# A graph-attention layer: adjacency pieces placed between the loads of x tiles, and the first table's rows stored from GpSimd's queue

## The chip, the cores and the metric

The kernel runs on one core of a Trainium2 chip. The metric is the device time of one execution in microseconds (us). A core has five engines with instruction queues of their own: TensorE (PE in the profile, its weight loads PEld), VectorE (DVE), ScalarE (ACT), GpSimd (POOL) and SyncE (SP). Each works through its queue in order. In this program SP, ACT and POOL also issue DMAs, which 16 shared DMA engines carry out. In the profile SPq and ACTq are the moments in which those queues issue a DMA.

## What is computed

The reference is one layer of graph attention with a residual and a layer norm, on x of 8 batches x 2048 nodes x 64 channels and one adjacency matrix of 2048 x 2048 for all batches, cut here to what matters:

```python
def _gat_layer(h, mask, b):
    scores = jnp.einsum('...nd,...md->...nm', h, h)
    scores = jnp.where(mask, scores, NEG)
    attn = jax.nn.softmax(scores, axis=-1)
    return jnp.einsum('...nm,...md->...nd', attn, h) + b
mask = graph + jnp.eye(N, dtype=graph.dtype) > 0
h = jnp.einsum('bnc,hdc->bhnd', x, Wh)                  # 4 heads of 64
out_h = _gat_layer(h, mask[None, None], bh[None, :, None, :])
z = leaky_relu(concat of the heads)
h2 = jnp.einsum('bnk,dk->bnd', z, Wo)
out2 = _gat_layer(h2, mask[None], bo)
x = layernorm(x + layernorm(leaky_relu(out2)) * gamma + beta)
```

The adjacency matrix is sparse. Only the first 32 nodes ("hubs") have many neighbours.

## The kernel before

`fast_kernel` works on the sparse matrix. (`general_kernel`, a dense version, runs only when a flag at the end says that a list of neighbours did not fit. It does not run here.) The nodes behind the 32 hubs are put into 168 sets of 12. For each set the kernel finds, on the chip, the nodes that any of the 12 is linked to, at most 128. It gathers their rows from a table in DRAM by an indirect DMA and does the attention of the set on them alone. The first attention layer gathers from `table1`, the second from `table2`, which the first one writes.

The work stands in three parts. The opening is from the start to about 142 us. The first layer runs over pairs of sets from there to about 640 us, and the second layer to the end. The change touches the opening, which does the following.

- **x tiles.** x is read in 16 tiles of 128 nodes with all 8 batches. `load_x(i)` (lines 462 to 467) sets two columns of ones on DVE and issues two DMAs of 128 KB from ACT's queue. `save_x(i)` (lines 469 and 470) stores the tile as 128 rows of 520 floats (260 KB) into `table1`, from ACT's queue too. Ten tile buffers go round.
- **Adjacency pieces.** `load_adj(r, t, m)` (lines 674 to 699) reads one piece: 120 rows (ten sets) by 1024 columns, by two or three DMAs from SP's queue, one of 440 KB and small ones (lines 681 and 682). POOL then turns the integers into a bf16 mask (line 687, about 1.1 us). After the second half m = 1 it sets the diagonal by small selects (lines 695 and 698). The raw integers use three buffers, the masks five. There are 34 pieces, in three rounds r of up to 60 sets. A piece is named below as round, ten and half. Where the round is 0 it is left out, so 5_1 is the second half of the sixth ten of round 0. `more(n)` issues the next n of them.
- **Hubs.** `hub_mask`, `hub_mask_sets`, `weights` and `hub_columns` prepare the hubs' masks and weights. In the x loop, `hub_scores(i)` computes the hubs' scores against tile i: matmuls (line 602), a subtraction of the mask on DVE (605) and an exponential on ACT (607). `turn_x(i + 1)` transposes the next tile on PE (525), and ACT copies it out (595). `hub_values(i - 1)` sums on PE (618). In step 3 POOL also sets a number of small tiles (lines 972 to 980) and builds the powers for a last short ten (`make_powers6`, line 713).
- **Picking neighbours.** `make_keys(r, t3, ...)` multiplies the masks of three tens by powers of two on PE (729), and DVE makes keys of them (718). Step 2 of the loop needs pieces 0_0 to 2_1 for it, step 6 pieces 3_0 to 5_1. From step 6 on, `pick(0)` hands out jobs to DVE, four in each step: MAX8 and match-replace (745, 747) pick the largest keys. `pick(0)` also issues, on POOL, a memset of the buffer `cand` (741), which the first MAX8 needs.
- **End of the opening.** After the loop come the keys of round 1 and the first six gathers on POOL (804), which need the whole of `table1`. Then `own_rows` runs on POOL, and the first matmul of the first layer (819, tile `cat`) at 142.05 us.

The order is written out by hand: under `manual_schedule` each engine gets its instructions in program order. Every DMA of SP and ACT carries one of eight completion semaphores, given out in rotation in program order. Before a DMA is issued its queue waits for the earlier user of that semaphore. DMAs of POOL have eight of their own. So a load of x waits for adjacency DMAs that stand some eight DMAs ahead of it in the program. While it waits, nothing behind it on ACT's queue runs.

The loop of the opening, before the change (lines 949 to 970):

```python
    more(6)
    hub_mask()
...
    turn_x(0)
    hub_columns()
    more(4)
...
    for i in range(NB):
        if i + 4 < NB:
            load_x(i + 4)
        more(1 if i >= 6 else 0)
        save_x(i)
```

Of the kernel before, what the change touches and what calls it, by code (L numbers as in the profile page):

```python
# [359 lines left out]
def fast_kernel(ctx: ExitStack, tc: tile.TileContext, x, adj, Wh, bh, Wo, bo, gamma, beta, out, flag):  # L360


    nc = tc.nc
    B, N, C = x.shape
    H, D, _ = Wh.shape
    P = 128
# [61 lines left out]
    table1 = dram.tile([N, ROW], F32, name="table1")  # L428
# [22 lines left out]
    xrow = {}  # L451
# [10 lines left out]
    def load_x(i):  # L462
        t = xrow[i] = rows_tile(f"x{i}")
        nc.vector.memset(t[:, :, 0:PW:PW - 1], 1.0)
        for p in range(2):
            nc.scalar.dma_start(out=t[:, :, 1 + p * D:1 + (p + 1) * D],
                                in_=x[p::2, i * P:(i + 1) * P, :].rearrange("q n c -> n q c"))

    def save_x(i):
        nc.scalar.dma_start(out=table1[i * P:(i + 1) * P, :], in_=xrow[i].rearrange("n q c -> n (q c)"))  # L470

    NCH = HALFN
    in_round = [min(FIRST, NS - FIRST * r) for r in range(NR)]
# [77 lines left out]
    def hub_mask():  # L551
        for k in range(2):
            nc.vector.tensor_scalar(hubm[:, k * NCH:(k + 1) * NCH], hubraw[k], 1.0, 0.0, OP.min, OP.max)
        nc.vector.tensor_tensor(hubm[:, :HUB], hubm[:, :HUB], identb[:HUB, :HUB], OP.max)
        pm = two("pm")
        for m in range(NB):
            nc.tensor.matmul(pm[:, m // 8, (m % 8) * HUB:(m % 8 + 1) * HUB], hubm[:, m * P:(m + 1) * P],
                             identb[:HUB, :HUB], start=True, stop=True)
        for k in range(2):
            nc.vector.tensor_scalar(  # L560
                maskh[:, k * 8:(k + 1) * 8, :].rearrange("p m (n h) -> p (m n) h", h=H),
                pm[:, k, :8 * HUB].unsqueeze(2).to_broadcast([P, 8 * HUB, H]), 0.0, 255.0, OP.is_equal, OP.mult)
        nc.vector.tensor_scalar(maskt[:HUB, NHB, :], pm[:HUB, 0, :HUB], 0.0, 255.0, OP.is_equal, OP.mult)
# [22 lines left out]
    def hub_columns():  # L586
        py = two("pyh")
        for h in range(H):
            nc.tensor.matmul(py[:, 0, h * P:(h + 1) * P], gram[:, h, :], xT[:, :, :HUB], start=True, stop=True)
        nc.vector.tensor_copy(yh.rearrange("p (m h) -> p m h", h=H), py[:, 0, :].rearrange("p (h m) -> p m h", h=H))  # L590

    def turn_x(i):
        tp = two(f"px{i}")
        turn(tp[:, 0, :], xrow[i])
        nc.scalar.copy(xT[:, :, i * P:(i + 1) * P], tp[:, 0, :].rearrange("c (q n) -> c q n", q=Q))

    def hub_scores(i):
        sp = two(f"sh{i}")
        for q in range(Q):
            for p in range(2):  # L600
                for r in range(2):
                    nc.tensor.matmul(sp[half(r), p, q * HW:(q + 1) * HW], xT[half(p), q, i * P + r * 64:i * P + (r + 1) * 64],
                                     yh[half(p), q * HW:(q + 1) * HW], start=True, stop=True)
        e = es[i % 2]
        nc.vector.tensor_tensor(e.rearrange("p (a q n) -> p a q n", a=2, q=Q), sp.rearrange("p a (q n) -> p a q n", q=Q),
                                maskh[:, i, :].unsqueeze(1).unsqueeze(1).to_broadcast([P, 2, Q, HW]), OP.subtract)
        nc.scalar.activation(e, e, AF.Exp, bias=shifts[:, 0:1], scale=1.0)
# [3 lines left out]
    def hub_values(i):  # L611

        for q in range(Q):
            for p in range(2):
                for u in range(2):
                    c0 = (p * Q + q) * HW + u * 64
                    o0 = q % 2 * PO + p * K1
                    nc.tensor.matmul(hubo[half(u), q // 2, o0:o0 + K1], es[i % 2][:, c0:c0 + 64], xrow[i][:, q, sums(p)],
                                     start=(i == 0 and q % 2 == 0 and p == 0), stop=(i == NB - 1), skip_group_check=True)
# [54 lines left out]
    def load_adj(r, t, m):  # L674

        s0 = FIRST * r + S10 * t
        ns = min(S10, NS - s0)
        np_ = ns * SET
        raw = early.tile([120, NCH], I32, tag="raw", name=f"raw{r}_{t}_{m}", bufs=3)
        for s, n0, n in flipped(s0, ns):  # L680
            nc.sync.dma_start(out=raw[s - s0:s - s0 + n], in_=adj[n0:n0 + n, m * NCH:(m + 1) * NCH])
        nc.sync.dma_start(out=raw[ns:np_], in_=byset[1:, s0:s0 + ns, m * NCH:(m + 1) * NCH])
        if m == 0:
            ahead[r, t] = early.tile([120, 2, HALFN + 80], BF16, tag="a", name=f"a{r}_{t}", bufs=5)
        a = ahead[r, t]
        w = NCH // 2
        nc.gpsimd.tensor_scalar(a[:np_, :, m * w:(m + 1) * w], raw[:np_].rearrange("p (c h) -> p h c", h=2),  # L687
                                1.0, 0.0, OP.min, OP.max)
        if m == 1:

            c1 = (REST + s0) // 2
            for h in range(2):
                for s, n0, n in flipped(s0, ns):
                    d = a[:np_, h, n0 // 2:(n0 + n) // 2]
                    nc.gpsimd.affine_select(out=d, in_=d, pattern=[[-2, n // 2]], base=s0 - s - h,
                                            channel_multiplier=1, compare_op=OP.not_equal, fill=1.0)
                d = a[:np_, h, c1:c1 + NS // 2 * (SET - 1)].rearrange("p (k c) -> p k c", k=SET - 1)[:, :, :ns // 2]
                nc.gpsimd.affine_select(out=d, in_=d, pattern=[[-ns, SET - 1], [-2, ns // 2]], base=-h - ns,
                                        channel_multiplier=1, compare_op=OP.not_equal, fill=1.0)
# [9 lines left out]
    def make_powers6():  # L709
        g = in_round[NR - 1] // S10 % 3  # L710
        d = powers6[:last * SET, g, 10 * g:10 * g + last]
        for k in range(SET):
            nc.gpsimd.affine_select(out=d, in_=d, pattern=[[-1, last]], base=-last * k, channel_multiplier=1,
                                    compare_op=OP.not_equal, fill=float(1 << k))
# [5 lines left out]
    def make_keys(r, t3, new):  # L720

        n = in_round[r]
        groups = [(t, min(S10, n - S10 * t)) for t in range(3 * t3, min(3 * t3 + 3, (n + S10 - 1) // S10))]
        pk = new(f"pk{r}_{t3}")
        for h in range(2):
            c = (2 * t3 + h) * 32
            for b in range(2):
                for i, (t, ns) in enumerate(groups):
                    nc.tensor.matmul(pk[c:c + 32, b, :], powers_of(ns, t % 3), ahead[r, t][:ns * SET, h, b * 512:(b + 1) * 512],
                                     start=(i == 0), stop=(i == len(groups) - 1), tile_position=(0, c))  # L730
        for h in range(2):
            part = slice((2 * t3 + h) * 32, (2 * t3 + h + 1) * 32)
            keep_keys(keys[r % 2][part, :], pk[part], part, h)
# [209 lines left out]
    def more(n):  # L943

        for _ in range(n):
            if pieces:
                load_adj(*pieces.pop(0))

    more(6)
    hub_mask()  # L950
    hub_mask_sets()
    weights()
    turn_x(0)
    hub_columns()
    more(4)
    picks = []

    def some(n):
        for _ in range(n):
            if picks:  # L960
                picks.pop(0)()
# [4 lines left out]
    for i in range(NB):  # L966
        if i + 4 < NB:
            load_x(i + 4)
        more(1 if i >= 6 else 0)
        save_x(i)  # L970
        if i == 3:
            nc.gpsimd.memset(rall[:, NG:, :], 1.0)
            nc.gpsimd.memset(rall2, 1.0)
            nc.gpsimd.memset(over, 0.0)
            for k in range(SET):
                nc.gpsimd.memset(bits[:, k:k + 1], N << k)
            nc.gpsimd.memset(shifts[:, 2:3], EPS)
            nc.gpsimd.memset(ones, 1.0)
            for t in rowts + xbs:
                nc.gpsimd.memset(t, 1.0)  # L980
            if last:
                make_powers6()
        hub_scores(i)
        if i + 1 < NB:
            turn_x(i + 1)
        if i:
            hub_values(i - 1)
        if i in (2, 6):
            make_keys(0, i // 6, two)
            if i == 2:  # L990
                more(2)
            if i == 6:
                picks = pick(0)
        some(4)
# [507 lines left out]
```

## Time and profile before

| what | us |
|---|---|
| median of 14 runs (lowest, highest) | 1034.72 (1026.79, 1038.19) |
| the profiled execution's own time | 1036.06 |
| its span in the trace | 1034.3 |
| PE busy, share of the span | 791.7, 77% |
| DVE busy | 605.6, 59% |
| ACT busy | 508.2, 49% |
| POOL busy | 506.4, 49% |
| first matmul of the first layer | 142.05 |
| mean granted TensorE clock | 0.917 |

The time of an execution is the span plus some 1.8 us around it. The page divides the span into 40 slices of 25.9 us and gives each engine's busy share in tenths for each slice. In the timeline a line has the start, the duration, the engine, the line of the kernel, the operation with its tiles, and in brackets how long the engine was idle before and what ended that. A group `x2` merges two instructions with the time between them. The view of waits has the total, the number of times and the longest. In the view of one line's instructions, three durations in ns are the minimum, the median and the maximum, and then follow the first and the last start.

### The profile page before, as it was taken

The page shows a single profiled execution, that of the slowest core. Times are in us where ns is not written, and L with a number is a line of the kernel's source. Part 1 is how long each engine was busy: PE and PEld are TensorE (multiplying, and loading weights), DVE is VectorE, ACT ScalarE, POOL GpSimd, SP SyncE. Part 2 cuts the span into 40 slices and gives each one's busy share as a digit, 9 for nine tenths or more (in the row PEclk, how much of TensorE's full clock was granted, in tenths as well). Part 3 has the DMA queues.
Part 4 walks back from the last instruction along what each step waited for, and adds up shares of the span by engine and source line. Part 5 has one row for each costly group of instructions (what it writes and reads, how often), then busy time and mean ns, then how long its engine had stood idle before and what let it go on. Part 6 is the DMA issues. An engine that isn't in the chain of part 4 may idle for free.

```text
span 1034.3 us, 42354 instructions
## 1 busy us (share of the span) xinstructions
PE 791.7 (77%) x18079; PEld 684.6 (66%) x18079; DVE 605.6 (59%) x1380; ACT 508.2 (49%) x1038; POOL 506.4 (49%) x718
## 2 busy tenths in 40 slices
PE   3266648999999999998999998329776667777760
PEld 3154547888899888887888887218666556556660
DVE  2038917789777777556656554002367656665895
ACT  2033225565666666655566674005446455555651
POOL 4364074844445555554566641751455555555203
PEclk9988879999999999998999998558899999999985
DMA  6588452433233344433344432853334555554311
GB/s 114 139 225 225 130 152 82 137 88 84 74 89 92 105 125 128 115 115 101 108 132 118 115 104 73 264 164 94 90 109 136 149 146 140 140 144 138 95 44 39
DMA packets 82208, 125.69 MB, mean 122 GB/s; under 512 B 35318, under 2 KB 51374, under 8 KB 82012
## 3 DMA queue, kind: packets, MB, share of 16 engines
q0 software_dynamic: 27424, 69.27, 24.8%
q1 hardware_dynamic: 34888, 44.85, 14.8%
q10 hardware_dynamic: 19700, 8.78, 3.7%
q8 instruction: 145, 2.38, 1.0%
q14 instruction: 51, 0.42, 0.1%
HBM read 124.98 MB, written 18.48 MB: 139 GB/s over the span
## 4 chain that ended last, share of the span: by engine, by line
PE 57%; issue 13%; DVE 10%; DMA 8%; ACT 7%; SPq 2%; another core or an unknown queue 1%; POOL 0%; ACTq 0%; DVEq 0%; POOLq 0%
PE s L834 9%; PE o L859 9%; PE bank L525 6%; PE t L525 6%; DMA raw<-in_adj_dram 5%; PE cat L819 5%; PE cat L544 4%; PE o L876 3%; PE cat L893 3%; ACT xts L1398 3%; PE bank L1264 2%; PE bank L1253 2%; PE o L1283 2%; PE cat L903 2%; DMA x<-in_x_dram 2%
## 5 line engine op out<-in xcount | busy, mean ns | idle before, releaser
L804 POOL DMA_INDIRECT g<-table,index x168 | 178.3, 1061 | 196.6 <-PE o L859 167.4
L804 POOL DMA_INDIRECT rows<-table,index x168 | 172.0, 1024 | 153.4 <-PE o L1283 91.8
L839 DVE TENSOR_TENSOR e<-s,mask 128x768 f32<-128x768 f32 x84 | 80.3, 956 | 102.1 <-PE s L834 101.1
L834 PE MATMUL s<-y,xTg 64*64 64x48 f32 x5376 | 117.4, 223 | 6.8 <-issue 4.6
L834 PEld LDWEIGHTS s<-y,xTg 64*64 64x64 f32 x5376 | 101.1, 135 | 27.0 <-issue 21.2
L525 PE MATMUL t<-ident,rows 128*128 128x128 f32 x672 | 93.2, 285 | 25.5 <-issue 25.1
L1398 ACT COPY xts<-t 128x1024 f32<-128x1024 f32 x84 | 81.3, 1010 | 53.4 <-PE t L525 41.8
L525 PEld LDWEIGHTS t<-ident,rows 128*128 128x128 f32 x672 | 80.5, 148 | 34.8 <-issue 34.4
L525 PE MATMUL bank<-ident,g 128*128 128x128 f32 x672 | 102.5, 276 | 0.0
L859 PE MATMUL o<-g,e 128*64 128x65 f32 x2688 | 101.3, 229 | 1.1 <-issue 0.9
L531 ACT ACTIVATE z<-cat,bhp 128x192 f32<-128x192 f32 x168 | 61.4, 417 | 74.0 <-PE cat L544 71.1
L859 PEld LDWEIGHTS o<-g,e 128*64 128x64 f32 x2688 | 88.9, 142 | 11.9 <-issue 2.4
L1152 ACT COPY xTg<-bank 128x512 f32<-128x512 f32 x168 | 90.2, 596 | 0.7 <-PE bank L525 0.6
L525 PEld LDWEIGHTS bank<-ident,g 128*128 128x128 f32 x672 | 81.8, 143 | 2.5 <-DVE keysi L773 0.6
L846 ACT ACTIVATE e<-e,shifts 128x768 f32<-128x768 f32 x84 | 81.1, 965 | 3.6 <-DVE e L839 3.6
L1253 PE MATMUL bank<-xts,share 128*32 128x128 f32 x1344 | 55.7, 283 | 35.1 <-issue 17.7
L825 ACT COPY y<-cat 128x384 f32<-128x384 f32 x80 | 41.0, 512 | 80.5 <-DVE rowt L907 50.4
L687 POOL TENSOR_SCALAR a<-raw 120x1024 bf16<-120x1024 int32 (+1 forms) x34 | 37.7, 1108 | 83.3 <-DMA raw<-in_adj_dram 42.8
L1253 PEld LDWEIGHTS bank<-xts,share 128*32 128x32 f32 x1344 | 38.6, 111 | 49.7 <-issue 44.6
L866 DVE RECIPROCAL rall<-o 64x8 f32<-64x8 f32 x168 | 34.5, 205 | 55.6 <-PE o L859 54.3
L819 PE MATMUL cat<-xo,gram 128*128 128x192 f32 x320 | 65.8, 328 | 0.0
L1283 PE MATMUL o<-rows,share 128*32 128x65 f32 x2688 | 54.7, 229 | 8.7 <-issue 4.5
(203 smaller groups left out, 1501.0 us busy)
## 6 DMA issues: line engine op xcount, KB each, us to landing
raw<-in_adj_dram SPq DMA_DIRECT2D x32, 440.0 KB
table<-xb SPq DMA_DIRECT2D x22, 256.0 KB
xr_s<-table SPq DMA_DIRECT2D x21, 256.0 KB
table<-x ACTq DMA_DIRECT2D x16, 260.0 KB
x<-in_x_dram ACTq DMA_DIRECT2D x32, 128.0 KB
table<-rowt SPq DMA_DIRECT2D x166, 24.4 KB
xb<-in_x_dram SPq DMA_DIRECT2D x168, 22.0 KB
out_dram<-y_s SPq DMA_DIRECT2D x144, 22.0 KB
```

Of the source, the lines that this page charges most:

```text
L525: nc.tensor.transpose(tp[:, q * P:(q + 1) * P], rows[:, q, 1:1 + P], ident)
L531: nc.scalar.activation(z[:, hp], cat[:, :, hp * n:(hp + 1) * n], AF.Identity, bias=bhp[:, hp:hp + 1], scale=1.0)
L804: nc.gpsimd.indirect_dma_start(out=t.rearrange("n q c -> n (q c)"), out_offset=None, in_=table, in_offset=bass.IndirectOffsetOnAxis(ap=(in ...
L819: nc.tensor.matmul(cat[:, k, 2 * GM:2 * GM + n], gram[:, g % 2 * 2 + k, :], held["x", g // 2][:, :n], start=True, stop=True)
L834: nc.tensor.matmul(sp[half(r), p, (q * 2 + j) * M:(q * 2 + j + 1) * M], xt[half(p), j, q, half(r)], y[half(p), (j * Q + q) * M:(j * Q + q ...
L839: nc.vector.tensor_tensor(e[:, :16 * M].rearrange("p (a q n) -> p a q n", a=2, q=Q), sp[:, :, :8 * M].rearrange("p a (q n) -> p a q n", q= ...
L846: nc.scalar.activation(e[:, :16 * M], e[:, :16 * M], AF.Exp, bias=shifts[:, 0:1], scale=1.0)
L859: nc.tensor.matmul(op[half(p), j, o0:o0 + K1], e[:, c0:c0 + 64], rw[j][:, q, sums(p)], start=True, stop=True)
L1152: nc.scalar.copy(t[:, k, :], bank[k])
L1253: nc.tensor.matmul(sp[q * 32:(q + 1) * 32, k, :], bd[u % 3][:, k, q, :], xt[:, s % 2, q, :], start=True, stop=True, tile_position=(0, q * 32))
L1283: nc.tensor.matmul(op[t * 32:(t + 1) * 32, f, k * W2 + p:k * W2 + p + K1], e[:, 2 * q + p, k, :], rw[:, q, sums(p)], start=(a == 0 and k = ...
L1398: nc.scalar.copy(t, tp)
```

## The change

Four edits in the opening:

1. Ahead of the x loop four adjacency pieces are issued instead of ten (6 + 4).
2. In steps 0 to 3 of the loop two pieces are issued each, between `load_x(i + 4)` and `save_x(i)`. With that, twelve are issued by the end of step 3 in place of step 2.
3. The two pieces that followed the first keys in step 2 are gone from there, since they are among those of step 3. The number and the order of the pieces stay the same.
4. `save_x(i)` issues its store from POOL's queue instead of ACT's, at its place in the program: behind the work on the pieces that were issued just before.

```diff
     def save_x(i):
-        nc.scalar.dma_start(out=table1[i * P:(i + 1) * P, :], in_=xrow[i].rearrange("n q c -> n (q c)"))
+        nc.gpsimd.dma_start(out=table1[i * P:(i + 1) * P, :], in_=xrow[i].rearrange("n q c -> n (q c)"))
...
-    more(6)
+    more(4)
     hub_mask()
     hub_mask_sets()
     weights()
     turn_x(0)
     hub_columns()
-    more(4)
...
     for i in range(NB):
         if i + 4 < NB:
             load_x(i + 4)
-        more(1 if i >= 6 else 0)
+        more(2 if i < 4 else 1 if i >= 6 else 0)
         save_x(i)
...
         if i in (2, 6):
             make_keys(0, i // 6, two)
-            if i == 2:
-                more(2)
```

## Prediction

> **What bounds the kernel now.** I read the page's slices first, to see where the engines stand idle, then the chain of waits for the first 150 us, then that stretch's timeline. The slices are 25.9 us each.
>
> ```profile
> PE   3266648999999999998999998329776667777760
> DVE  2038917789777777556656554002367656665895
> DMA  6588452433233344433344432853334555554311
> ```
>
> PE is busy two to six tenths in the first six slices and nine tenths from slice 8 on. So the first 142 us (the x loop and the picking of neighbours, up to the first `cat` matmul at 142.05) are a stage of its own with other limits than the body. This is the chain of waits through it:
>
> ```profile
> by line: DMA raw<-in_adj_dram 34.0%; issue 26.5%; DMA x<-in_x_dram 10.6%; DMA table<-x 5.4%; POOL a L687 3.1%; PE bank L525 1.8%; DVE share L718 1.6%; PE sh L602 1.3%; PE pk L729 1.2%; PE cat-4_1520 L819 1.1%; PE cat-3_1525 L819 1.1%; ACT e
> ```
>
> Half of the chain is transfers. Where they stop the engines stands in the timeline (start, duration, instruction, idle time before it and what ended it):
>
> ```profile
> 27.13 1.23 DVE L605 TENSOR_TENSOR e<-sh,maskh 128x1024 f32<-128x1024 f32 x1 [2.09 <-PE sh L602]
> ...
> 37.28 4.08 ACTq L466 DMA_DIRECT2D x<-in_x_dram  x2
> ...
> 41.58 0.35 ACTq L470 DMA_DIRECT2D table<-x  x1
> 42.05 1.15 ACT L607 ACTIVATE e<-e,shifts 128x1024 f32<-128x1024 f32 x1 [19.95 <-DMA x<-in_x_dram]
> ```
>
> Step 0's scores are ready on DVE at 28.36, but ACT takes their exponential only at 42.05. Between them in ACT's queue stand the two loads of x tile 4 and the store of row tile 0. The built program's order shows why they wait: eight completion semaphores are shared in rotation by all DMAs of SP and ACT, and a DMA waits for the earlier one on its semaphore. The loads of tile 4 stand behind ten adjacency pieces in the program, so they wait for two DMAs of piece 2_0, which landed at 41.15. So it goes on, as ACT's waits from 0 to 142 us show (total, times, longest):
>
> ```profile
> ACT e L607 <- DMA x<-in_x_dram: 35.0, 4, 19.9
> ACT e L607 <- DVE e L605: 33.7, 9, 7.3
> ```
>
> Step 6 comes at 78.71. From then on DVE is the bound: 2.4 to 2.9 us of each 3 us from 84 to 126, with four picking jobs of 0.98 us and a 1.2 us subtraction in each step.
>
> ```profile
> 74.45 0.31 POOL L741 MEMSET share<- 128x256 f32 x1
> ...
> 82.89 0.43 DVE L745 MAX8 share<-share 128x8 f32<-128x256 f32 x1
> ...
> 133.69 1.12 POOL L804 DMA_INDIRECT g<-table,index  x1 [0.48 <-DVE rall L625]
> ```
>
> From the first MAX8 (82.89) to the first gather (133.69) pass 50.8 us. So the question is when the first MAX8 can start.
>
> **The change, part by part.**
>
> *ACT's queue.* The 16 stores leave it (0.33 to 0.99 us each to issue, plus their waits). By the changed program's order the loads of tile 4 now wait for piece 1_0, whose predecessors are untouched and which POOL converted at 27.78. So step 0's exponential runs at about 28.4 instead of 42.05. The loads of tile 5 wait for piece 2_0. In the changed order piece 1_1 goes into the buffer of the first hub rows (read by DVE at 4.0) and no longer waits for POOL to convert piece 1_0. It is issued right behind 1_0 and lands 3.7 later (the gap of the pair 2_0 and 2_1 now: 41.15 to 44.86), at 31.5; piece 2_0 follows 3.6 behind, at 35.1. Step 1's exponential: 35.5 (now 51.44). Steps that met little took 4.18 us (63.41 to 67.59) to 5.05 (51.44 to 56.49), 4.6 in the mean, and the step with the first keys 6.92 (56.49 to 63.41). So step 6 comes at 35.5 + 4 x 4.6 + 6.92 = 60.8 instead of 78.71, and the first MAX8 could follow 4.18 later (78.71 to 82.89 now): 65.0.
>
> *Adjacency pieces.* The second keys, ahead of MAX8, need piece 5_1. From 2_0 (41.15) to 5_1 (66.23) seven pieces took 3.58 us each. From 1_1 at 31.5, eight more at that pace give 60.1. The DMA engines were 84% busy from 42 to 66 us; if they were full, the pace would be 3.0 and 5_1 would come at 55.5. I take the middle, 57.8. With conversion and selects (66.23 to 68.17 now, 1.94) the piece is usable at 59.7, in time for step 6.
>
> *GpSimd's queue.* Here is the new wait. MAX8 also waits for POOL's memset of `cand` (L741), which today ends at 74.76, 8.1 us before it is needed. In the changed order stand between 5_1 and it: the store of tile 3, the memsets and the powers (68.17 to 73.42: 5.25), the stores of tiles 4 and 5, one conversion (1.03) and the store of tile 6. The trace has no such store. POOL's plain DMAs of 22 KB take 0.56 to 0.67 us; its gathers, which move the same 128 rows of 520 floats, 0.94 to 2.04:
>
> ```profile
> L1366 POOL DMA_DIRECT2D out_dram<-y_s x12: 558/577/672, 1009.2 to 1025.8; - x12
> ...
> L804 POOL DMA_INDIRECT g<-table,index x168: 998/1038/2039, 133.7 to 610.7; - x168
> ```
>
> I take the gathers' usual 1.0 us, since rows and bytes are the same. That gives 59.7 + 1.0 + 5.25 + 2.0 + 1.03 + 1.0 + 0.31 = 70.3 for the memset's end, later than the 65.0 of the x loop. **First MAX8 at 70.4, 12.5 earlier than 82.89.** Stores 0 to 2 fall into POOL's waits for pieces (0.8 to 3.7 us each from 42 to 66 now) and cost nothing; without that cover each would add its 1.0. Behind a blocked store would stand the conversions, behind these SP's next pieces, and behind those the keys.
>
> Two sections of the Trainium skill speak against the move. "DMA: Bandwidth & Descriptors", section on SWDGE vs HWDGE vs iDMA, sends plain transfers to SP or ACT, because GpSimd writes descriptors in software. "SBUF — State Buffer", section "SBUF: two separate sides", adds that VectorE's two-port copies lock GpSimd out, with 620 ns grown to about 3100 in its example. By that figure four stores would cost an estimated 8.4 us more, and the run 1032.0. The gathers' rows here show no more than 2.04, with DVE at work beside them.
>
> *After MAX8.* The 50.8 us to the first gather are DVE's jobs, which the change leaves alone. Ten adjacency pieces at 3.58 (36 us) fit in, so do the x tiles, loaded four steps ahead. The first gather also waits for all stores; the last stands behind the conversion of piece 4_1 of round 1, which now runs at 104.45, 29 us ahead of the gather. So they are hidden, and the body behind 142 us moves as a whole.
>
> **Sum.** The profiled execution took 1036.06 (span 1034.3): less 12.5 is 1023.6. The median of the 14 runs is 1034.72; less 12.5 is 1022.2. I give **1023.0**. Between the ends, pace 3.0 and stores of 0.56 give 12.5 + 2.3 + 1.8 = 16.6 of gain; pace 3.58 and stores of 2.04 give 12.5 - 2.3 - 4.2 = 6.0. From the two bases that is 1018.1 to 1030.1.
>
> **Rivals.**
>
> *GpSimd takes half the gain back* (1030): stores as long as the slowest gather, and pieces no faster than now. For it: POOL becomes last ahead of MAX8 anyway. Against: the median gather is 1.04.
>
> *The stage is held by transfers all the same* (1035): pieces or tiles fall behind after step 6, and the early start is waited away before the first gather. For it: the DMA engines are 65 to 98% busy from 42 to 114 us. Against: from 114 to 132 they stand below 25%, so there are some 15 us to shift into. That the change does nothing at all is excluded by the changed order of loads and semaphores.
>
> *GpSimd becomes the bound, slower than before.* One mechanism: each store holds POOL while DVE works beside it. The four stores between 5_1 and the memset eat the gain when 4 x (c - 1.0) passes 12.5, that is from c = 4.1 us. At c = 5 the four cost 16 more, and stores 0 to 2, longer than the 4 us that POOL idles per two pieces (2 x 3.58, less 3.2 of conversions and selects), add 1 each: 1036.06 - 12.5 + 16 + 3 = 1042.6. Against: no DMA instruction on POOL took over 2.04.
>
> **Numbers.** Forecast (gain of 8 us and more) 0.70; half the gain 0.13; held by transfers 0.08; GpSimd the bound 0.09. A measurement of this kernel tells about 0.3% from no change (3.1 us). So faster 0.83, within 0.3% 0.08, slower 0.09. The range takes the first two cases with the bounds of their unknowns: 1017 to 1031.
>
> **What would show it.** Right: step 0's exponential at 28 to 29, step 6 near 61, L470 on POOL at about 1.0 us, the first MAX8 near 70 with POOL's L741 as what ended DVE's wait, and the first gather some 51 us behind it. Wrong: a step 0 that still waits 10 us for a load; conversions late behind stores; DVE with gaps between 85 and 120; or L470 above 2 us.

## The result, and the profile after

The changed kernel takes 1025.72 us (median of 10 runs, 1020.59 to 1028.87), against 1035.41 for the kernel before in the same rounds (47 runs). The ratio is 0.9909, with a 95% interval of 0.9886 to 0.9933: some 9 us faster. The profiled execution took 1027.36 (span 1025.6), 8.7 less than the 1036.06 before.

The slices of 25.6 us each, from the page of the changed kernel:

```profile
PE   3747578999999999998899998219877677677850
DVE  2349627798777767565556554001367756666894
DMA  6888243422233434443344432853344545555311
```

Slices 2 to 4 show the move: DVE stands at 3, 4, 9 where it was at 0, 3, 8, and DMA at 8, 8, 8 instead of 5, 8, 8. Work that used to wait for the first 42 us has moved forward. The body keeps its pattern.

The chain of waits over 0 to 150 us, the changed kernel:

```profile
by line: DMA raw<-in_adj_dram 32.3%; issue 27.2%; DMA x<-in_x_dram 9.2%; POOL a L687 2.5%; DVE e L605 2.5%; PE bank L525 2.2%; PE s L834 2.0%; DVE share L747 2.0%; DVE share L745 1.8%; POOL powers L713 1.5%; PE sh L602 1.4%; PE pk L729 1.2%
```

`DMA table<-x` (5.4% before) is gone from it, and `POOL powers L713` is new: GpSimd's preparations now stand on the path. The timeline says where (start, duration, instruction, idle time before and what ended it):

```profile
24.13 4.11 ACTq L466 DMA_DIRECT2D x<-in_x_dram  x2
27.92 1.23 DVE L605 TENSOR_TENSOR e<-sh,maskh 128x1024 f32<-128x1024 f32 x1 [2.09 <-PE sh L602]
29.25 1.15 ACT L607 ACTIVATE e<-e,shifts 128x1024 f32<-128x1024 f32 x1 [6.36 <-DMA x<-in_x_dram]
...
60.34 1.15 ACT L607 ACTIVATE e<-e,shifts 128x1024 f32<-128x1024 f32 x1 [2.75 <-DVE e L605]
61.99 0.57 POOL L470 DMA_DIRECT2D table<-x  x1
...
68.19 1.10 POOL L470 DMA_DIRECT2D table<-x  x2 [0.29 <-issue]
70.35 0.57 POOL L470 DMA_DIRECT2D table<-x  x1
70.92 0.33 POOL L741 MEMSET share<- 128x256 f32 x1
71.28 0.43 DVE L745 MAX8 share<-share 128x8 f32<-128x256 f32 x1 [5.64 <-POOL share L741]
```

The two loads of x tile 4 still hold ACT's queue, but only until 28.2 instead of 41.4, so step 0's exponential runs at 29.25, right behind its scores on DVE (27.92 + 1.23). Step 6 comes at 60.34 instead of 78.71. The first MAX8 then waits 5.64 us for the memset of `cand`, behind four stores. It starts 11.6 us earlier than at 82.89. ACT's waits from 0 to 142 us show the same:

```profile
ACT e L607 <- DVE e L605: 45.4, 11, 14.0
ACT e L607 <- DMA x<-in_x_dram: 8.9, 2, 6.4
ACT e L607 <- DMA raw<-in_adj_dram: 5.0, 1, 5.0
```

35.0 us of waiting behind loads of x have become 8.9, or 13.9 with step 1's wait of 5.0: the view names an adjacency DMA for it, but the loads of tile 5 stand ahead of that exponential in ACT's queue. The wait for DVE (14.0 in one piece) is now step 7, which stands behind the late MAX8.

### The profile page after: what moved, and what is told of

It is laid out like the page before. It is cut to its first block, busy times and chain, and to the rows that moved or that the text cites. A ratio compares the mean times of both kernels' runs of the same rounds, so it can differ in the third digit from the quotient of the medians.

```text
span 1025.6 us, 42370 instructions
## 1 busy us (share of the span) xinstructions
PE 782.7 (76%) x18079; PEld 674.3 (66%) x18079; DVE 605.5 (59%) x1380; ACT 508.1 (50%) x1038; POOL 516.3 (50%) x734
## 4 chain that ended last, share of the span: by engine, by line
PE 56%; issue 12%; DVE 12%; DMA 7%; ACT 6%; another core or an unknown queue 3%; SPq 2%; POOL 1%; ACTq 0%; DVEq 0%; POOLq 0%
PE s L834 9%; PE o L859 9%; PE t L525 6%; PE bank L525 6%; DMA raw<-in_adj_dram 5%; PE cat L819 4%; PE cat L544 3%; PE o L876 3%; ACT xts L1395 3%; PE cat L893 2%; PE bank L1250 2%; PE bank L1261 2%; PE o L1280 2%; PE cat L903 2%
## 5 line engine op out<-in xcount | busy, mean ns | idle before, releaser
L525 PE MATMUL t<-ident,rows 128*128 128x128 f32 x672 | 95.9, 287 | 15.8 <-issue 14.0
L525 PEld LDWEIGHTS t<-ident,rows 128*128 128x128 f32 x672 | 80.8, 149 | 26.0 <-issue 25.6
L867 DVE TENSOR_TENSOR osb<-o,rall 128x512 f32<-128x512 f32 x84 | 58.1, 692 | 2.9
```

The lines of the kernel that those rows point to most:

```text
L525: nc.tensor.transpose(tp[:, q * P:(q + 1) * P], rows[:, q, 1:1 + P], ident)
L867: nc.vector.tensor_tensor(osb, v[:, :, :, 1:K1], r.unsqueeze(3).to_broadcast([P, 4, 2, D]), OP.mult)
```

## The experiments

Theory at the outset: both edits free ACT's queue, and the first MAX8 then waits for GpSimd. Rivals: the order of the pieces alone does it; the queue alone does it; GpSimd or the transfers take the gain back. Each ratio is to the kernel before in the same rounds, since its median differs: 1035.41 us beside the changed kernel, 1029.8 beside `e1` to `e4` and 1034.4 beside the others. The last three columns are starts in one profiled execution.

| kernel | ratio, 95% interval | step 6 | first MAX8 | first gather |
|---|---|---|---|---|
| before | 1 | 78.71 | 82.89 | 133.69 |
| the changed kernel | 0.9909 (0.9886 to 0.9933) | 60.34 | 71.28 | 123.91 |
| order alone, `e1_order_only` | 0.9873 (0.9839 to 0.9908) | 63.53 | 67.89 | 118.97 |
| queue alone, `e2_stores_only` | 0.9992 (0.9977 to 1.0008) | 75.60 | 80.96 | 137.15 |
| `cand` early, `e3_cand_early` | 0.9880 (0.9854 to 0.9906) | 61.07 | 66.40 | 121.78 |
| quarter stores, `e4_quarter_stores` | 0.9996 (0.9969 to 1.0023) | 62.52 | 77.05 | 129.52 |
| stores on SP, `e5_sp_stores` | 0.9877 (0.9842 to 0.9912) | 61.01 | 69.08 | 120.24 |
| preparations early, `e9_preps_early` | 0.9870 (0.9848 to 0.9893) | 61.99 | 67.38 | 121.61 |
| the same, stores on ACT, `e10_preps_early_act` | 0.9879 (0.9852 to 0.9906) | 63.77 | 67.72 | 119.69 |
| that and gathers first, `e11_preps_act_gathers` | 0.9773 (0.9745 to 0.9801) | 66.11 | 71.44 | 112.64 |
| changed kernel again, `r1_after_again` | 0.9897 (0.9857 to 0.9936) | 61.71 | 70.65 | 123.06 |
| order alone again, `r2_order_again` | 0.9898 (0.9861 to 0.9935) | 65.89 | 70.53 | 123.12 |
| changed, gathers first, `e7_gathers_first` | 0.9843 (0.9801 to 0.9884) | 60.42 | 70.85 | 112.40 |
| order alone, gathers first, `e12_order_gathers` | 0.9828 (0.9790 to 0.9866) | 66.51 | 71.00 | 112.69 |

### Each half alone

`e1_order_only` keeps the new order and puts the stores back on ACT. `e2_stores_only` keeps the old order and moves only the stores.

```diff
 e1: the changed kernel with
-        nc.gpsimd.dma_start(out=table1[i * P:(i + 1) * P, :], ...)
+        nc.scalar.dma_start(out=table1[i * P:(i + 1) * P, :], ...)
 e2: the kernel before with
-        nc.scalar.dma_start(out=table1[i * P:(i + 1) * P, :], ...)
+        nc.gpsimd.dma_start(out=table1[i * P:(i + 1) * P, :], ...)
```

> The changed order of the pieces, with the row stores left on ACT's queue. Theory (order and queue share the gain, the order has most of it): step 0's exponential still comes at 28 to 30, but a store in ACT's queue keeps the loads behind it and shares their semaphores, so that step 2 waits for a piece again (some 44 instead of 40.1), step 6 comes at about 64 instead of 60.3, and the first gather at 125 to 127: 1026 to 1030. Rival 'the order alone': as the changed kernel or better, since GpSimd has four stores of 0.57 us fewer ahead of the first MAX8: 1022 to 1025.7. Rival 'the queue alone': step 0's exponential at about 42 and 1035.

> The old order of the pieces, with the row stores on GpSimd's queue. Theory: step 0's exponential still waits until some 40 to 42 for the loads of x tile 4, since those stand behind the same ten pieces; step 6 comes near 75 to 79, and the stores then stand ahead of GpSimd's preparations: first gather at 134 to 139, 1035 to 1041. Rival 'the queue alone': step 0's exponential at 29 and 1026 to 1030.

The order alone gave as much as the whole change: 0.9873, the range of its rival, with the first gather at 118.97 and not at the 125 to 127 of the theory. The queue alone gave nothing: 0.9992, with step 6 and the first gather where its theory had them. Its timeline shows the old wait still there, and what happens later:

```profile
41.81 1.15 ACT L607 ACTIVATE e<-e,shifts 128x1024 f32<-128x1024 f32 x1 [18.93 <-DMA x<-in_x_dram]
...
104.28 4.03 ACTq L466 DMA_DIRECT2D x<-in_x_dram  x2
108.36 1.15 ACT L607 ACTIVATE e<-e,shifts 128x1024 f32<-128x1024 f32 x1 [5.21 <-DMA raw<-in_adj_dram]
...
130.69 3.32 PE L729 MATMUL pk<-a,powers 120*32 120x512 bf16 x12
```

Step 0's exponential still waits 18.93 us for the loads of tile 4. Later three pairs of loads hold ACT's queue for 3.4 to 4.0 us each and the exponentials of steps 8, 10 and 11 with it (the last is shown), so the 1.9 us won at MAX8 (82.89 to 80.96) are lost again: DVE has written the index at 125.46 instead of 123.59. The matmuls `pk` then take 3.32 us instead of 1.92, and the first gather comes 3.5 us later than before. What held these late loads was not tried.

The pair shows that the order decides. That the shared semaphores are the link is read from the program. The landings agree: in the changed kernel the loads of tile 4 end at 28.24, piece 1_0 is converted at 27.99, the loads of tile 5 end at 35.83 and 2_0 is converted at 35.04. No run changed the semaphores themselves.

### The place of the stores, in the same rounds

`e1` at 0.9873 and the changed kernel at 0.9909 came from different rounds, and two profiles of one kernel can differ. So both were run once more together, unchanged.

> The changed kernel itself, on the same chip and in the same rounds as the order alone. It decides whether moving the stores from ACT's queue to GpSimd's gains or costs. If the move costs (GpSimd's stores, preparations and conversions ahead of the first MAX8 cost more than ACT saves), this run lies 2 us or more above the order alone, near 0.991 of the kernel before. If the two places are equal, both lie at 0.987 to 0.990, within 1.5 us of each other.

> The order of the pieces alone, stores on ACT, beside the changed kernel on one chip. If the move of the stores costs: 0.9873 again, 2 us or more under the changed kernel, first MAX8 near 68 and first gather near 119. If the places are equal: within 1.5 us of the changed kernel.

The medians are 1023.71 and 1024.34 us, the ratios 0.9897 and 0.9898: no difference can be told. The intervals reach some 4 us to each side. The reading that the move costs 5 us, taken from `e1` alone, is not borne out. The two timelines show how they come to the same end in this pair. The changed kernel:

```profile
61.71 1.15 ACT L607 ACTIVATE e<-e,shifts 128x1024 f32<-128x1024 f32 x1 [2.55 <-DVE e L605]
70.65 0.43 DVE L745 MAX8 share<-share 128x8 f32<-128x256 f32 x1 [4.32 <-POOL share L741]
```

The order alone:

```profile
65.89 1.15 ACT L607 ACTIVATE e<-e,shifts 128x1024 f32<-128x1024 f32 x1 [5.33 <-DMA x<-in_x_dram]
70.53 0.43 DVE L745 MAX8 share<-share 128x8 f32<-128x256 f32 x1 [1.27 <-POOL share L741]
```

With the stores on GpSimd, step 6 comes 4.2 us earlier, but MAX8 then waits 4.32 for the memset behind the stores. With the stores on ACT the x loop is slower, and the memset is late by only 1.27. In this pair, what ACT saves, GpSimd spends ahead of the same instruction. (`e1`, the order alone too, had its MAX8 at 67.89 in its profile.) `e5_sp_stores` puts them on SP's queue (`nc.sync` in the same line):

> The changed kernel with the row stores on SP's queue, among the adjacency pieces. GpSimd then has no store and ACT neither. If a store's wait for its row tile (written by DVE a step earlier) holds up no piece, step 6 comes at 60 to 61, MAX8 at 67 to 68.5, the first gather at 118 to 120, ratio 0.986 to 0.988. If it does, pieces come 2 to 4 us later from step 4 on, and the first gather at 122 to 126, ratio 0.989 to 0.994.

It gave 0.9877, MAX8 at 69.08 and the first gather at 120.24: the case in which a store holds up no piece, if half a microsecond late. Its interval overlaps those of the other two places, though it comes from other rounds: between the three queues no difference can be told.

### What a store on GpSimd costs, and where that decides

```diff
-        nc.gpsimd.dma_start(out=table1[i * P:(i + 1) * P, :], in_=xrow[i]...)
+        for k in range(4):
+            nc.gpsimd.dma_start(out=table1[i * P + k * 32:i * P + (k + 1) * 32, :],
+                                in_=xrow[i][k * 32:(k + 1) * 32]...)
```

> The changed kernel, with each row store as four DMAs of 32 rows on GpSimd's queue, the same bytes. It prices the rival 'GpSimd becomes the bound'. If a DMA costs GpSimd by its number, a store takes 4 x 0.57 = 2.3 us; the four ahead of the memset of cand delay it by 7 us at least, pieces are converted later, and the first gather comes at 131 to 145: 1033 to 1047. If the cost goes by rows and bytes, a quarter takes about 0.15 us and the time is that of the changed kernel, 1025.7.

The instructions of line 470 in the changed kernel (three durations, then first and last start), and two stores with the first MAX8 in `e4`:

```profile
L470 POOL DMA_DIRECT2D table<-x x16: 547/572/584, 40.4 to 102.4; - x16
```

```profile
69.53 4.09 POOL L471 DMA_DIRECT2D table<-x  x8 [0.31 <-issue]
...
77.05 0.43 DVE L747 MAX8 share<-share 128x8 f32<-128x256 f32 x1 [9.93 <-POOL share L743]
```

A store holds GpSimd for 0.57 us, with little spread. As four DMAs of the same bytes it takes 2.0 us (4.09 for two stores): the cost goes by the number of DMAs. The four stores ahead of the memset delay MAX8 by 4 x 1.44 = 5.8, from 71.28 to 77.05, and the first gather by 5.6. The whole gain is gone at 0.9996, some 9 us above the changed kernel's 0.9909. The opening explains 5.6 of these. The remainder lies inside the intervals and is not settled.

### What comes after an earlier MAX8

`e3` moves the memset of `cand` to the start. `e9`, whose diff follows, moves it and all of step 3's preparations to behind the first adjacency piece, where GpSimd waited 5.2 us. `e10` is `e9` with the stores on ACT.

```diff
-    more(4)
+    more(1)
+    nc.gpsimd.memset(rall[:, NG:, :], 1.0)
...
+        make_powers6()
+    nc.gpsimd.memset(cand, 0.0)
+    more(3)
...
-        if i == 3:
-            nc.gpsimd.memset(rall[:, NG:, :], 1.0)
...
```

> The changed kernel, with the memset of cand moved to the start of the program. Theory (the first MAX8 waits for GpSimd's preparations, and the stage behind it follows it): MAX8 starts at 65 to 67 instead of 71.28, and the first gather follows 2.5 to 5 us earlier than 123.91: 1021 to 1023. Rival (behind MAX8 the stage is held by adjacency transfers or by GpSimd's conversions): MAX8 earlier, the first gather within 1 us of 123.91 and 1025 to 1026.

> The changed kernel (stores on GpSimd), with GpSimd's memsets, the powers and the memset of cand moved from step 3 to behind the first adjacency piece, where GpSimd waited 5.2 us for data. The order alone (stores on ACT) had its first gather at 118.97 and 0.9873 of the kernel before; the changed kernel 123.91 and 0.9909. Theory (the stores cost because they meet GpSimd's preparations in one queue ahead of the first MAX8): with these gone, MAX8 comes at 64 to 66, conversions from tile 4 on 4 to 6 us earlier than in the changed kernel, first gather at 115 to 119, ratio 0.980 to 0.986. Rival (stores on GpSimd cost wherever they stand, or adjacency pieces hold the steps): MAX8 at 66, first gather at 121 to 123, ratio 0.988 to 0.991.

> The same early preparations with the stores on ACT's queue (only the order of the pieces from the change). By the theory the two places of the stores then differ by little: MAX8 waits for the x loop alone (step 6 at 63.5, DVE free at 65.8), so it starts at 65.8 to 67 instead of 67.89, the first gather at 116.5 to 118.5, ratio 0.984 to 0.987, within 2 us of the same kernel with stores on GpSimd. By the rival it stays 3 us or more ahead of that kernel.

MAX8 came at 66.40 in `e3` and 67.38 in `e9`, and no longer waits for GpSimd: 4 to 5 us earlier than 71.28. The first gather came only 2.1 and 2.3 us earlier (121.78, 121.61), and the ratios 0.9880 and 0.9870 overlap that of the changed kernel. For `e9` the rival's gather (121 to 123) came true, the theory's (115 to 119) did not, and the ratio stands between the two. `e10` had its MAX8 at 67.72 and its gather at 119.69, both later than the theory said, and at 0.9879 it is not told from `e9`. In `e9` steps 7 and 8 show what gives the time back:

```profile
72.08 1.15 ACT L607 ACTIVATE e<-e,shifts 128x1024 f32<-128x1024 f32 x1 [8.46 <-DVE e L605]
...
74.03 6.38 ACTq L466 DMA_DIRECT2D x<-in_x_dram  x2
...
80.46 1.15 ACT L607 ACTIVATE e<-e,shifts 128x1024 f32<-128x1024 f32 x1 [6.76 <-DVE x L464]
```

Step 8 follows 8.4 us behind step 7 instead of the usual 5.06, because two loads of x hold ACT's queue for 6.38 us. It looks like the wait at 37.28 in the kernel before, eight tiles later. `e3` has one at step 9, which follows 7.25 us behind step 8. `e10`, with the stores on ACT, has none: its steps 7 to 10 come at 72.41, 77.47, 81.90 and 86.34. So an early MAX8 alone does not bring this wait. Which DMA the loads waited for was not tried.

### The gathers first

In the changed kernel's timeline, the end of the opening:

```profile
117.45 3.30 PE L729 MATMUL pk<-a,powers 120*32 120x512 bf16 x12
...
120.32 2.16 POOL L687 TENSOR_SCALAR a<-raw 120x1024 bf16<-120x1024 int32 x2 [17.33 <-PE pk L729]
...
123.91 1.11 POOL L804 DMA_INDIRECT g<-table,index  x1 [0.57 <-DVE rall L625]
```

GpSimd stands idle for 17.33 us until matmuls free a mask buffer, converts two pieces of round 1, and only then gathers, though DVE has written the index at 112.2. These three kernels put the six gathers ahead:

```diff
     hub_values(NB - 1)
-    make_keys(1, 0, two)
-    more(2)
     while picks:
         picks.pop(0)()
...
     own_rows(0)
     own_rows(1)
+    make_keys(1, 0, two)
+    more(2)
     hub_end()
```

> Early preparations, stores on ACT, and the first six gathers ahead of the keys and pieces of round 1, which they stood behind: GpSimd waits 16 us for the matmuls pk before it converts two pieces, then gathers, though the index is ready at 108. If the opening ends with the gathers' place in GpSimd's queue, the first gather comes at 106 to 110, the first cat 8.4 behind it, ratio 0.974 to 0.980. If round 1's keys and picks are what the body needs first, the gain comes back within the first 60 us of the body, and the ratio is that of the kernel without this edit, 0.984 to 0.987.

> The changed kernel with the first six gathers (and their own rows) ahead of the keys and pieces of round 1. With early preparations and stores on ACT the same edit gave 0.9879 to 0.9773. If its gain is its own (the gathers stood behind pk and two conversions in GpSimd's queue), it takes about 11 us here too: first gather at 112 to 115, ratio 0.978 to 0.982. If it needs GpSimd free of stores, the gathers wait for the last store as well, and half of the gain is left: 0.984 to 0.987.

> The order of the pieces alone, stores on ACT, preparations in step 3, with the six gathers first. If the early preparations gave nothing, this is the best version: first gather at 108 to 112, ratio 0.974 to 0.978. If the early preparations matter with it, it stays behind 0.9773 by 0.003 or more.

`e12`'s timeline has the two in the new order:

```profile
112.69 1.24 POOL L804 DMA_INDIRECT g<-table,index  x1 [11.67 <-PE sh L602]
...
121.70 2.16 POOL L687 TENSOR_SCALAR a<-raw 120x1024 bf16<-120x1024 int32 x2
```

The first gather comes at 112.4 to 112.7 in all three, 7 to 10.7 us earlier than without the edit. (That is later than the 106 to 112 expected of `e11` and `e12`: their step 6 came at 66.11 and 66.51 in these profiles, not at 63.5.) The ratio falls by 0.0106 (`e11` against `e10`), 0.0070 (`e12` against `r2`) and 0.0054 (`e7` against `r1`). Stores on GpSimd do not hold the gathers in `e7` (the last is issued at 102.1). Its 0.9843 lies in the range of the smaller gain, though its gather does what the larger one said; the interval spans both. The opening of `e12` and `e11` ends at the same time (first `cat` at 121.19 and 121.40), and whether early preparations matter beside it stays open. All three ratios lie under the changed kernel's, but the intervals of `e7` and `e12` still touch those of the same kernels without the edit, and only `e11`'s stands clear. The best is `e11` at 0.9773 (0.9745 to 0.9801): 1012.30 us against 1034.42.

## Why the prediction was right, and where it was not

The predicted 1023.0 stands against a measured 1025.72. The steps, by the profiled execution (1036.06 - 11.6 + 1.8 + 1.1 = 1027.36):

- **Step 0 freed: right.** 29.25 against 28.4. Piece 1_1 was converted at 31.62 (said 31.5), 2_0 at 35.04 (35.1), step 1 ran at 35.87 (35.5), step 6 at 60.34 (60.8). `e1` and `e2` show the cause: with the order alone step 0 came at 30.71, with the queue alone at 41.81.
- **Pieces' pace: at the slow end.** 5_1 came at 60.05 instead of 57.8. The pace was (60.05 - 31.62) / 8 = 3.55 us, about the 3.58 of the kernel before. Halfway to 3.0 assumed that half of the DMA engines' free share would be used, but they were 86% busy in that stretch, against 84% in the row it was worked out from: 2.25 us late.
- **A store on GpSimd: 0.57 us, not 1.0.** The plain DMAs of 22 KB (558/577/672 ns) were the right row, not the gathers with the same bytes, and `e4` shows why: the cost goes by the number of DMAs. The four stores took 1.7 less than said.
- **First MAX8 behind the memset: right.** 71.28 against 70.4, with `<-POOL share L741` on the line. That the number came so close is in part luck: the late pieces and the short stores nearly cancel.
- **MAX8 to the first gather: 52.63 instead of 50.8.** 1.4 of the 1.8 us is one group of matmuls, `pk`: 3.30 us against 1.92 before. The granted TensorE clock at that place differs (below). The prediction called the whole stretch DVE's jobs. DVE had written the index 10.1 us ahead of the first gather in the kernel before (123.59) and 11.7 in the changed one (112.20). What stood between was `pk` and two conversions in GpSimd's queue, and the three kernels with the gathers first took most of it away.
- **The body unchanged: right within its spread.** From the first gather to the end it took 901.7 against 900.6. Over the other profiles this stretch was 890.8 to 906.4, so the 1.1 us lies inside its spread. With such a spread a forecast within 3 us of the median owes something to luck too.

What failed is the credit to the second edit. "The 16 stores leave it" stood as part of the gain, and the sum had the cost on GpSimd without asking what the order alone would give. With and without the move the ratio is 0.9897 and 0.9898 in the same rounds: the second half of the change does nothing to the time that these intervals can tell.

The rivals: "GpSimd takes half the gain back" had the pace right (no faster than before) and the stores wrong (0.57 us, not 2.04). "GpSimd becomes the bound" was set to decide from 4.1 us a store. Its mechanism was real: in `e4`, with stores of 2.0 us, MAX8 moved by the 4 x 1.44 of its four stores. By the opening that leaves a gain of 4 us at the first gather, but the ratio of 0.9996 shows none, and this difference stays open. "Held by transfers" did not hold the changed kernel. In `e3` and `e9` late loads of x took back a part of the next step, in `e10` they did not.

The Trainium skill, page "DMA: Bandwidth & Descriptors", section on SWDGE vs HWDGE vs iDMA, sends plain transfers to SP or ACT. Here GpSimd, ACT and SP gave 0.9897, 0.9898 and 0.9877, the last in other rounds, with no loss on GpSimd that the intervals show. The page "SBUF — State Buffer", section "SBUF: two separate sides", has a GpSimd DMA grow from 620 to 3100 ns beside a DVE copy. No store took more than 584 ns here, with DVE 62% busy from 40 to 102 us. Almost all of its work there was MAX8, match-replace and operations that read PSUM. Two short copies took 1.0 us, and the one store beside them 0.57, so that the case of the page was hardly met.

## What to carry to other kernels

When DMAs of several queues share completion semaphores in program order, look at what stands ahead of a load in the program, not only in its queue: moving six pieces behind the loads gave as much as the whole change. When a change moves work from one queue to another, follow both queues to the next instruction that needs both; here it was one memset, and the move gained nothing that could be measured. Run each half of a two-part change alone, and in the same rounds.

## What the runs showed of the hardware that was not expected

- **The granted clock differs between profiles at the same place.** It was low at the last matmuls ahead of the gathers in one profile and full in another. The windows (engines' busy time, then the granted clock, the DMA share and GB/s) around `pk`, in the changed kernel and then in the kernel before:

```profile
116.00:120.00 4.00, 3.85 (x43) 2.13 (x44) 0.86 (x3) 0.10 (x1) 0.00 (x0) 0.62 0.00 0
```

```profile
126.00:130.00 4.00, 2.46 (x43) 1.71 (x44) 2.18 (x7) 1.15 (x1) 0.00 (x0) 1.00 0.00 2
```

  The twelve matmuls took 3.30 us at 0.62 and 1.92 us at 1.00. In the order alone they took 1.92 in one profile and 3.03 in the other, so the queue of the stores does not decide it. What does is not shown.
- **One kernel's opening differs by 4 us between profiles.** The order alone had its first gather at 118.97 in one profile and at 123.12 in another. From `e1` beside the changed kernel one would have read that the stores on GpSimd cost 5 us. The pair in the same rounds showed no difference.
